# Moving the raw weight loads of a two-level fast matmul from SyncE's DMA queue to ScalarE's

## The chip, the cores and the metric

The kernel runs on one core of one Trainium2 chip. The metric is the device time of one execution in microseconds, as a median over runs. TensorE (PE) multiplies, VectorE (DVE) adds and reads PSUM, ScalarE (ACT) copies out of PSUM and applies relu, GpSimd (POOL) adds in SBUF, SyncE (SP) issues nearly all DMAs. DMAs can also be issued from ACT.

## The reference, cut to what matters

Two residual layers on `x` of shape 2 x 2048 x 512, all in fp32. The first is a mixture: two shared experts and, for each of the two samples, one chosen expert out of five, each 512 to 2048 to 512 with a relu; a softmax gate over three weights, computed from the first token, mixes the three. The second is one chosen 512 x 512 matrix per sample.

```
s0, s1 = relu(x @ swi[0]) @ swo[0], relu(x @ swi[1]) @ swo[1]
h  = relu(einsum('bsd,bdf->bsf', x, wi[type_label]))
eo = einsum('bsf,bfd->bsd', h, wo[type_label])
w  = softmax(relu(concat([eo[:,0], s0[:,0], s1[:,0]]) @ g1) @ g2)
x  = x + eo*w[:,0] + s0*w[:,1] + s1*w[:,2]
x  = x + einsum('bsd,bdh->bsh', x, W[cat_ids]) + b[cat_ids]
```

## The kernel before, in words

**Units.** There are 12 units of work in order: shared expert 0 on four blocks of 1024 tokens, shared expert 1 on the same four blocks, then chosen expert 2 (sample 0) on blocks 0 and 1, and chosen expert 3 (sample 1) on blocks 2 and 3. A unit is an `up` matmul (512 to 2048, line L810) and a `down` matmul (2048 to 512, L945). Both use a seven-product scheme in place of eight, on two levels, so 49 products each. An `up` has 98 slots (seven outer products i, each with seven inner products k in two halves); a `down` has 49. A slot is a few matmuls, the PSUM read that they call for, and whatever background work the slot advances. `clock` counts slots.

**Weight sums.** A product needs sums of weight blocks. For each expert and each of the two matrices (`Prep(e, kind)`, experts 1 to 3, so six of them; expert 0's are made in the first unit) these sums are made once, in four slices. A slice is read as raw weights into the one buffer tagged `raw` (1 MB, eight DMAs of 128 KB, L186); then POOL makes twelve additions (L141) in three lines of four: `o` and `s` read the raw slice, `t` reads `s`. After each addition POOL runs two small memsets (L149). Five slots after a line's fourth addition the line is stored to HBM (`ws_o`, `ws_s`, `ws_t`, L236). The next slice begins when all eight readers of `raw` have been issued and five slots have passed (`free`), and its additions may begin six slots after that (`can`). In an `up` the additions are spread by `RATE_UP` additions a slot, with at most four saved up; in a `down` they go at fixed places (`RUN_DN`), and there POOL first waits for a small DVE memset (`pulse`, L691, and `seen`, L692). `prep_paced` is called once in every slot and counts `clock`.

**Weight tiles.** `fetch_w` loads each product's 256 KB weight tile (`w`) from HBM into twelve rotating buffers. Every load is an SP DMA, issued in program order when a slot has used up a tile: from `ws_t` (L485), `ws_s` (L487), `ws_o` (L489) or the given weights (L494 to L504). The SP queue therefore holds, in one order, the weight tiles, the raw slices, the stores of the sums and the activations' parts.

**Evictions.** A product of the first inner index leaves its PSUM bank by an ACT copy or a DVE addition (`uz`, L825 and L827; `us`, L831 and L833; `h`, L838 to L857), and the next inner product adds to the same bank, so PE has to wait for that read. At places DVE makes wide sums of 128 x 1024 (L787 in `up`, L916 in `down`, L744 to L751 for both).

**Start.** `read_ids` loads the two label vectors by DMA and reads each into an SP register (L91, L93). It stands, in program order, behind the first four transposed pieces of `x` (ACT copies, L286) and the loads of the first weights, and ahead of the first `up`. The whole program is issued in the order it is written; each engine runs its own part in that order.

Of the kernel before, what the change touches and what calls it, by code (L numbers as in the profile page):

```python
# [36 lines left out]
def cond_resid_kernel(  # L37
# [22 lines left out]
    nc = tc.nc  # L60
    B, S, D = x.shape
    E, _, F = wi.shape
    NCAT = W.shape[0]
    NX = g2.shape[1]
    DC = D // P
# [15 lines left out]
    ps = ctx.enter_context(tc.tile_pool(name="ps", bufs=2, space=PSUM))  # L81
    dram = ctx.enter_context(tc.tile_pool(name="dram", bufs=1, space=DRAM))

    label, cat = [], []

    def read_ids():
        ids = const.tile([1, 2, B], type_label.dtype, name="ids")
        nc.sync.dma_start(out=ids[:, 0, :], in_=type_label.rearrange("(o b) -> o b", o=1))
        nc.sync.dma_start(out=ids[:, 1, :], in_=cat_ids.rearrange("(o b) -> o b", o=1))
        for b in range(B):  # L90
            label.append(nc.sync.value_load(ids[0:1, 0, b : b + 1], min_val=0, max_val=E - 1))  # L91
        for b in range(B):
            cat.append(nc.sync.value_load(ids[0:1, 1, b : b + 1], min_val=0, max_val=NCAT - 1))  # L93

# [5 lines left out]
    wi_v = wi.rearrange("e (c p) (r f) -> p (e c) r f", p=P, r=4)  # L100
    swi_v = swi.rearrange("e (c p) (r f) -> p (e c) r f", p=P, r=4)
    wo_v = wo.rearrange("e (r g p) d -> p (e r) g d", p=P, g=NG)
# [28 lines left out]
    def sums_a(eng, pick, put):  # L131


        a11, a12, a21, a22 = pick(0, 0), pick(1, 0), pick(0, 1), pick(1, 1)
        for o, i0, i1, op in (
            (put(5), a21, a22, ADD),
            (put(7), a11, a21, SUB),
            (put(6), put(5), a11, SUB),
            (put(3), a12, put(6), SUB),
        ):  # L140
            eng.tensor_tensor(o, i0, i1, op)  # L141
            yield
# [3 lines left out]
    def rest(count):  # L146

        for _ in range(count):
            nc.gpsimd.memset(idle, 0.0)  # L149

    class Prep:
# [4 lines left out]
        def __init__(self, e, kind):  # L156
# [2 lines left out]
            self.left = {part: NG for part in "ost"}  # L159
            self.p, self.late, self.reading, self.free, self.since = [], [], 0, 0, 0  # L160

        def begin(self):
            if not self.todo:
                return
            g = self.todo.pop(0)
            self.since = clock[0]
            e, kind = self.e, self.kind
            t = bigp.tile([P, 2048], F32, tag="raw", bufs=1, name=f"pr_{e}_{kind}_{g}")

            raw = t.rearrange("p (q b d f) -> p q b d f", q=4, b=2, d=2)  # L170
            cols = slice(g * P, (g + 1) * P)
            for c in range(DC):
                if kind == 0 and e < 2:
                    src = swi_v[:, e * DC + c, :, cols]
                elif kind == 0:
                    src = wi_v[:, bass.ds(label[e - 2] * DC + c, 1), :, cols]
                    src = src.rearrange("p o r f -> p (o r) f")
                elif e < 2:
                    src = swo_v[:, e * 4 + c, g, :].rearrange("p (r f) -> p r f", r=4)
                else:  # L180
                    src = wo_v[:, bass.ds(label[e - 2] * 4 + c, 1), g, :]
                    src = src.rearrange("p o (r f) -> p (o r) f", r=4)
                src = src.rearrange("p (c d) f -> p c d f", c=2)
                a, b = divmod(c, 2)
                for k, q in enumerate((1, 2) if a else (0, 3)):
                    nc.sync.dma_start(out=raw[:, q, b, :, :], in_=src[:, k, :, :])  # L186
            place = lambda n: SLOT_A[n] - 4
            quad = {(0, 0): 0, (1, 0): 1, (1, 1): 2, (0, 1): 3}
            own = {}

            def view(part):
                if part not in own:
                    self.flush(1 << 30, part)
                    own[part] = bigp.tile(
                        [P, 1536 if part == "o" else 2048], F32, tag=part, bufs=1,
                        name=f"p{part}_{e}_{kind}_{g}",
                    )
                form = {
# [3 lines left out]
                }[part]  # L202
                return own[part].rearrange(form, s=4, f=P, **({"b": 2} if part == "s" else {}))

            def line(part, pick, put):
                gen = sums_a(nc.gpsimd, pick, put)

                def op(k):
                    next(gen)
                    rest(2)  # L210
                    if part != "t":
                        self.reading -= 1
                        self.free = clock[0] + 5
                    if k == 3:
                        self.late.append((clock[0] + 5, part, g, own[part]))

                return [lambda k=k: op(k) for k in range(4)]

            self.p += line(
                "o", lambda r, c: raw[:, 0:3, r, c, :], lambda n: view("o")[:, :, place(n), :]  # L220
            )
            self.p += line(
                "s", lambda r, c: raw[:, quad[r, c]], lambda n: view("s")[:, place(n)]
            )
            self.p += line(
                "t", lambda r, c: view("s")[:, :, r, c], lambda n: view("t")[:, :, place(n)]
            )
            self.reading = 8

        def flush(self, now, only="ost"):  # L230
            for job in list(self.late):
# [7 lines left out]
                )  # L239
                self.left[part] -= 1  # L240

        def step(self):

            self.flush(clock[0])
            done = self.can()
            if done:
                self.p.pop(0)()
            self.more()
            return done

        def can(self):
            return bool(self.p) and (len(self.p) != 12 or clock[0] >= self.since + 6)

        def more(self):
            if self.reading == 0 and (not self.p or clock[0] >= self.free):
# [5 lines left out]
        def force(self, part):  # L261
            self.more()
            while self.left[part]:
                if self.p:
                    self.p.pop(0)()
                self.more()
                if not self.p:
                    self.flush(1 << 30)
# [184 lines left out]
    clock = [0]  # L453
# [194 lines left out]
    prep_bg, other_bg = [], []  # L648
# [9 lines left out]
    def prep_step():  # L658
        done = prep_bg[0].step()
        if prep_bg[0].over():  # L660
            prep_bg.pop(0)
        return done
# [3 lines left out]
    def prep_paced(rate):  # L666
        clock[0] += 1
        if prep_bg:
            prep_bg[0].flush(clock[0])
        pace[0] = min(pace[0] + rate, 4.0) if prep_bg else 0.0  # L670
        while prep_bg and pace[0] >= 1 and prep_step():
            pace[0] -= 1
# [81 lines left out]
    def up(n, xg, tops, y):  # L754
# [12 lines left out]
        for j, i in enumerate(I_UP(n)):  # L767
# [32 lines left out]
            for s, (bk, k, d) in enumerate(SEQ_UP):  # L800
# [78 lines left out]
                if s in top_at:  # L879
                    next(tg, None)  # L880
                prep_paced(RATE_UP[n in MAKES][j])
                if n or j or s >= 7:
                    step(other_bg)
# [10 lines left out]
    def down(n, H, tops, y, prepare):  # L894
# [124 lines left out]
        for s, (i, name) in enumerate(SLOTS_DN):  # L1019
            if s in at:  # L1020
                for _ in job:
                    pass
                job = jobs[at[s]]()
                y_sums(0, *sums.get(at[s], ()))
            elif s in second:
                y_sums(1, *sums.get(second[s], ()))
            slot(i, name)
            next(job, None)
            if name == "z2" and i != 1:
                next(job, None)  # L1030
            prepare(s)
            prep_paced(0.0)
            prep_run(RUN_DN[n in MAKES].get((i, name), 0))
            quiet[0] = True
            step(other_bg)
# [220 lines left out]
    def last_layer1(blk, y):  # L1256
# [8 lines left out]


    RATE_UP = [
        [0.36, 0.36, 0.36, 0.36, 0.24, 0.24, 0.36],
        [0.0, 0.24, 0.24, 0.3, 0.3, 0.3, 0.3],
    ]  # L1270
    RUN_DN = [
# [5 lines left out]
    with tc.manual_schedule():  # L1277
# [9 lines left out]
        next(x_rest)  # L1287
        begin = First(y)
        read_ids()
        xg = x_sums(0)  # L1290
        advance(xg)
# [4 lines left out]
        for n, (e, blk) in enumerate(units):  # L1296
# [47 lines left out]
            if e >= 2:  # L1344
                b = e - 2
# [41 lines left out]
```

## Time and profile before

| what | value |
|---|---|
| time, median of 3 runs | 2229.15 us (2228.36 to 2230.01) |
| the profiled execution | 2225.8 us, its span 2224.0 us |
| PE busy / DVE / ACT / POOL | 2184.7 / 1627.8 / 544.3 / 811.9 us |
| moved by DMA | 581.59 MB, 262 GB/s over the span |
| raw slice loads | 192 of 128 KB, all from SP, between 166.0 and 1480 us |
| loads issued from ACT | 25, all of `x` |

Times are microseconds from the span's start. A "waits" row reads: engine and line that waited, what released it, the total, how often, the longest. A timeline row reads: start, duration, engine (SPq and ACTq are the DMA issues of SP and ACT), line, operation, tiles, count, and in brackets the idle time before it with its releaser. A row of the windows reads: stretch, length, busy time and instruction count of PE, weight loads, DVE, ACT and POOL, the granted TensorE clock, the DMA engines' share and GB/s. Unit 0 ends at 212 us, unit 4's `up` begins at 728 us, and the last addition on a weight slice starts in unit 8, at 1548.9 us.

### The profile page before, as it was taken

The numbers are of one execution on the slowest core, as the hardware profiler recorded it, in microseconds if no ns is written. First come the engines' busy times: TensorE is split into PE (matmuls) and PEld (weight loads), VectorE is DVE, ScalarE is ACT, GpSimd is POOL, SyncE is SP. The second block draws the span as 40 slices with busy tenths as digits, with TensorE's granted clock in tenths as the row PEclk, the third lists the DMA queues.
The fourth block names the chain that finished last, engine by engine and source line by source line (L and its number), as shares of the span: only waits on it lengthen the run. The fifth ranks groups of instructions, "written<-read, shape, count | busy, mean of one in ns | idle before, by whom it ended". The sixth has DMA issues, their size and how long they took to land.

```text
span 2224.0 us, 29253 instructions
## 1 busy us (share of the span) xinstructions
PE 2184.7 (98%) x9808; PEld 1851.8 (83%) x9808; DVE 1627.8 (73%) x2047; ACT 544.3 (24%) x937; POOL 811.9 (37%) x1259
## 2 busy tenths in 40 slices
PE   8999999999999999999999999999999999999999
PEld 6787888888888888888888888888877877887785
DVE  7897787687587587588587588588676746867695
ACT  3221231331321321231231141131133133213310
POOL 5887533852840540450450451360033023002400
PEclk9999999999999999999999999999999999999999
DMA  9853997997996996896997997896896697679681
GB/s 341 319 178 98 340 326 218 340 328 233 298 306 211 316 315 200 285 328 185 294 316 223 302 302 236 272 337 205 298 297 192 185 314 237 183 236 318 215 282 52
DMA packets 484256, 581.59 MB, mean 262 GB/s; under 512 B 28552, under 2 KB 316296, under 8 KB 480908
## 3 DMA queue, kind: packets, MB, share of 16 engines
q1 hardware_dynamic: 480380, 572.91, 79.4%
q10 hardware_dynamic: 3728, 6.82, 0.9%
q8 instruction: 80, 1.31, 0.2%
q14 instruction: 68, 0.56, 0.1%
HBM read 421.80 MB, written 157.81 MB: 261 GB/s over the span
## 4 chain that ended last, share of the span: by engine, by line
PE 85%; DVE 7%; DMA 2%; issue 1%; SPq 0%; ACT 0%; DVEq 0%; ACTq 0%
PE dx L945 23%; PE ux L810 23%; PE dy L945 11%; PE uy L810 11%; PE dz L945 6%; PE uz L810 6%; PE po L1159 5%; DVE h L916 1%; DMA w<-ws_t 1%; DVE h L787 1%; DVE t L749 1%; DMA w<-in_L_cond_W_dram 1%; DVE t L747 1%; DVE t L744 1%; DVE t L751 0%
## 5 line engine op out<-in xcount | busy, mean ns | idle before, releaser
L810 PE MATMUL ux<-xs,w 128*128 128x256 f32 x1792 | 426.2, 380 | 10.0 <-DVE uz L827 5.0
L945 PE MATMUL dx<-t,w 128*128 128x256 f32 x1680 | 397.4, 379 | 3.3 <-DVE ds L967 3.1
L810 PEld LDWEIGHTS ux<-xs,w 128*128 128x128 f32 x1792 | 338.9, 190 | 69.8 <-DVE uz L827 8.0
L945 PEld LDWEIGHTS dx<-t,w 128*128 128x128 f32 x1680 | 318.1, 190 | 48.7 <-issue 2.4
L1196 POOL TENSOR_TENSOR mix<-mix 128x512 f32<-128x512 f32 x72 | 110.1, 1531 | 443.0 <-ACT mix L1191 355.3
L833 DVE TENSOR_TENSOR us<-ux,h 128x512 f32<-128x512 f32 x240 | 163.2, 687 | 128.3 <-PE ux L810 128.0
L916 DVE TENSOR_TENSOR h<-h,h 128x1024 f32<-128x1024 f32 x192 | 246.4, 1297 | 0.0
L781 ACT ACTIVATE h<-h 128x1024 f32<-128x1024 f32 x156 | 163.9, 1054 | 235.0 <-DVE h L838 122.4
L810 PE MATMUL uy<-xs,w 128*128 128x256 f32 x896 | 212.5, 380 | 2.1 <-DVE h L857 1.9
L838 DVE TENSOR_TENSOR h<-uy,us 128x512 f32<-128x512 f32 x168 | 116.0, 691 | 119.6 <-ACT us L831 115.5
L692 POOL TENSOR_TENSOR seen<-pulse 1x1 f32<-1x1 f32 x33 | 16.9, 513 | 509.7 <-DVE pulse L691 473.2
L810 PEld LDWEIGHTS uy<-xs,w 128*128 128x128 f32 x896 | 169.7, 190 | 30.0 <-DVE h L857 4.3
L844 ACT ACTIVATE h<-uz 128x512 f32<-128x512 f32 x168 | 99.5, 592 | 351.4 <-PE uz L810 312.2
L945 PE MATMUL dy<-h,w 128*128 128x256 f32 x672 | 159.7, 381 | 4.2 <-DVE y L969 4.1
L810 PE MATMUL ux<-xi,w 128*128 128x256 f32 x640 | 152.2, 380 | 5.1 <-DVE us L833 2.9
L945 PEld LDWEIGHTS dy<-h,w 128*128 128x128 f32 x672 | 127.4, 190 | 22.8 <-issue 5.2
L945 PE MATMUL dx<-h,w 128*128 128x256 f32 x616 | 145.5, 379 | 0.0
L945 PE MATMUL dz<-h,w 128*128 128x256 f32 x616 | 145.5, 379 | 0.0
L857 DVE TENSOR_TENSOR h<-uy,us 128x512 f32<-128x512 f32 x168 | 112.1, 686 | 44.0 <-PE uy L810 42.2
L810 PEld LDWEIGHTS ux<-xi,w 128*128 128x128 f32 x640 | 120.5, 190 | 25.1 <-issue 7.2
L141 POOL TENSOR_TENSOR po<-pr 128x384 f32<-128x384 f32 x48 | 54.5, 1136 | 232.5 <-DMA pr<-in_L_cond_wo_dram 82.4
L787 DVE TENSOR_TENSOR h<-h,h 128x1024 f32<-128x1024 f32 x96 | 135.4, 1410 | 3.2 <-ACT h L844 1.9
(155 smaller groups left out, 3432.9 us busy)
## 6 DMA issues: line engine op xcount, KB each, us to landing
w<-ws_t SPq DMA_DIRECT2D x352, 256.0 KB, 4.2
w<-ws_s SPq DMA_DIRECT2D x270, 256.0 KB, 4.2
w<-ws_o SPq DMA_DIRECT2D x264, 256.0 KB, 4.6
xs<-xs SPq DMA_DIRECT2D x56, 896.0 KB, 7.4
ws_s<-ps SPq DMA_DIRECT2D x24, 1024.0 KB, 8.1
ws_t<-pt SPq DMA_DIRECT2D x24, 1024.0 KB, 9.5
ys<-y SPq DMA_DIRECT2D x11, 2048.0 KB, 7.8
ws_o<-po SPq DMA_DIRECT2D x24, 768.0 KB, 6.6
```

Source lines behind the costliest of these rows:

```text
L141: eng.tensor_tensor(o, i0, i1, op)
L781: nc.scalar.activation(v, v, AF.Relu)
L787: nc.vector.tensor_tensor(o, blk_of(O[22], cc), blk_of(O[21], cc), ADD)
L810: nc.tensor.matmul(p[:, g, :], lhsT=wt[:, 2 * d + g, :], rhs=x_ops[n, i, k], start=first and g == 0, stop=True, skip_group_check=True,)
L833: nc.vector.tensor_tensor(t, p, half(src, 12 if k == 6 else 22, d), ADD)
L838: nc.vector.tensor_tensor(half(dst, 22, d), bank["y", d], t, ADD)
L844: nc.scalar.activation(half(dst, 11, d), p, AF.Relu if i in final else AF.Copy)
L857: nc.vector.tensor_tensor(half(dst, 12, d), p, sn["b", d], ADD)
L916: nc.vector.tensor_tensor(bl(o), bl(i0), bl(i1), SUB)
L945: nc.tensor.matmul(p, lhsT=wt[:, g, :], rhs=op[g], start=first and g == 0, stop=True, skip_group_check=True,)
L1159: nc.tensor.matmul(po[t], lhsT=mixed[c], rhs=l1[blk][0][:, c, :], start=(c == 0), stop=(c == DC - 1),)
L1196: nc.gpsimd.tensor_tensor(m[:, 3, :, :], m[:, 3, :, :], m[:, j, :, :], ADD)
```

## The change

The eight loads of every slice are no longer issued when the slice begins. They are put on a list, and `prep_paced` issues one of them in each slot, from ACT's DMA queue. This goes for the slices of shared expert 1 as for those of the chosen experts. Because the addresses depend on the labels, ACT reads the type labels into registers of its own at the start. A slice's additions may begin once the list is empty and four slots have passed since its last load. `RATE_UP` rises by 0.02 from unit 4 on (its first row; units 1 to 3 use the second, which stays).

```diff
     def read_ids():
...
         for b in range(B):
-            label.append(nc.sync.value_load(ids[0:1, 0, b : b + 1], min_val=0, max_val=E - 1))
+            of = ids[0:1, 0, b : b + 1]
+            label.append(nc.sync.value_load(of, min_val=0, max_val=E - 1))
+            label_act.append(nc.scalar.value_load(of, min_val=0, max_val=E - 1))
...
         def begin(self):
...
-                    src = wi_v[:, bass.ds(label[e - 2] * DC + c, 1), :, cols]
+                    src = wi_v[:, bass.ds(label_act[e - 2] * DC + c, 1), :, cols]
...
-                    src = wo_v[:, bass.ds(label[e - 2] * 4 + c, 1), g, :]
+                    src = wo_v[:, bass.ds(label_act[e - 2] * 4 + c, 1), g, :]
...
                 for k, q in enumerate((1, 2) if a else (0, 3)):
-                    nc.sync.dma_start(out=raw[:, q, b, :, :], in_=src[:, k, :, :])
+                    self.loads.append((raw[:, q, b, :, :], src[:, k, :, :]))
...
+        def load(self):
+            if self.loads:
+                o, v = self.loads.pop(0)
+                nc.scalar.dma_start(out=o, in_=v)
+                self.since = clock[0]
...
         def can(self):
-            return bool(self.p) and (len(self.p) != 12 or clock[0] >= self.since + 6)
+            if len(self.p) == 12:
+                return not self.loads and clock[0] >= self.since + 4
+            return bool(self.p)
...
         def force(self, part):
             self.more()
             while self.left[part]:
+                while self.loads:
+                    self.load()
...
     def prep_paced(rate):
         clock[0] += 1
         if prep_bg:
             prep_bg[0].flush(clock[0])
+            prep_bg[0].load()
...
     RATE_UP = [
-        [0.36, 0.36, 0.36, 0.36, 0.24, 0.24, 0.36],
+        [0.38, 0.38, 0.38, 0.38, 0.26, 0.26, 0.38],
         [0.0, 0.24, 0.24, 0.3, 0.3, 0.3, 0.3],
     ]
```

More of the change, by code (lines that the diff above doesn't have):

```diff
@@ L82, in cond_resid_kernel @@
     dram = ctx.enter_context(tc.tile_pool(name="dram", bufs=1, space=DRAM))
-    label, cat = [], []
+    label, label_act, cat = [], [], []
     def read_ids():
@@ L160, in __init__ @@
             self.p, self.late, self.reading, self.free, self.since = [], [], 0, 0, 0
+            self.loads = []
         def begin(self):
```

## The prediction

> **What bounds the kernel now.** I began with the page's busy shares and the chain that ended last, from which these lines are taken.
>
> ```profile
> PE 2184.7 (98%) x9808; PEld 1851.8 (83%) x9808; DVE 1627.8 (73%) x2047; ACT 544.3 (24%) x937; POOL 811.9 (37%) x1259
> ...
> PE 85%; DVE 7%; DMA 2%; issue 1%; SPq 0%; ACT 0%; DVEq 0%; ACTq 0%
> ```
>
> PE is the bound: no change of loads can bring more than PE's idle time, 2224.0 - 2184.7 = 39.3 us, and only the part near the moved loads. So I cut the span at the borders of the stages (columns as in the table's notes).
>
> ```profile
> 0.00:212.00 212.00, 191.44 (x852) 160.10 (x853) 182.08 (x183) 54.87 (x103) 154.39 (x141) 0.98 0.68 240
> 212.00:728.00 516.00, 515.53 (x2418) 452.67 (x2417) 376.65 (x484) 128.70 (x230) 251.30 (x476) 1.00 0.87 284
> 728.00:1510.00 782.00, 771.82 (x3558) 673.85 (x3557) 577.46 (x721) 188.91 (x309) 292.07 (x565) 1.00 0.88 281
> ```
>
> PE is idle 20.6 us in unit 0, 0.5 us in units 1 to 3 (9 of the 24 slices are loaded up to there, at no cost) and 10.2 us from 728 us to 1510 us, where the other loads lie. PE's waits in that last stretch:
>
> ```profile
> PE ux L810 <- DVE uz L827: 3.5, 5, 1.1
> PE ux L810 <- DMA w<-ws_t: 2.3, 2, 1.9
> PE ux L810 <- DMA w<-in_L_cond_swi_dram: 2.2, 1, 2.2
> PE uy L810 <- DVE h L857: 1.9, 2, 1.1
> ```
>
> 4.5 us are late weight tiles, 5.4 us are late DVE evictions. One of the late tiles, first on SP's queue, then on PE:
>
> ```profile
> 938.94 0.52 SPq L236 DMA_DIRECT2D ws_s<-ps  x1
> 939.67 10.10 SPq L186 DMA_DIRECT2D pr<-in_L_cond_wo_dram  x8
> 949.87 0.38 SPq L485 DMA_DIRECT2D w<-ws_t  x1
> ```
>
> ```profile
> 953.63 0.67 PE L810 MATMUL ux<-xs,w 128*128 128x256 f32 x2 [1.92 <-DMA w<-ws_t]
> ```
>
> The tile is issued only when the eight raw loads have left SP, and PE waits for it. The bursts before the other two late tiles (0.4 us at 783.3, 2.2 us at 1135.1) also held SP about 10 us: from 769.5 to 779.6 and from 1115.9 to 1125.6.
>
> **What leaves SP.** A burst that nothing obstructs takes SP 4.15 us (1475.89, eight issues with a median of 0.33 us and what lies between). In a 10 us burst the other 6 us are its first issue (6.29 us at 939.67), and that wait belongs to the 1 MB store ahead of it: where a tile stands behind such a store it has it too (w<-ws_o, 6.50 us at 953.80, behind ws_t<-pt). So this part stays on SP and goes to the next tile; about 4.1 us a burst leave. The three tiles were late by 0.4, 1.9 and 2.2 us, less than 4.1 each. Gain 4.5 us, between 0 (the bytes, not the issue, are late) and 4.5.
>
> The Trainium skill speaks against the change here: "DMA: Bandwidth & Descriptors", under "Issuing engines are not separate DMA queues", says that DMAs from any engine share the same 16 DMA engines and that a second issuer saves only the issuing time. The DMA share of 0.88 beside the 10 us burst agrees that the engines are nearly full; by the strictest reading of the rule the tiles land as late as before and this term would be 0, by the issue rows it is 4.5.
>
> **What ACT gets.** 192 loads and some register instructions. The nearest row is ACT's own loads of `x`: 24 issues, 0.334 to 0.444 us, median 0.335, so 192 x 0.335 = 64 us on an engine that is busy 24%. They need not wait for SP's blocked queue:
>
> ```profile
> 318.72 4.02 SPq L487 DMA_DIRECT2D w<-ws_s  x1
> ...
> 322.46 0.33 ACTq L300 DMA_DIRECT2D xn<-in_x_dram  x1
> ```
>
> A load stands behind its slot's eviction and runs while that is computed; what is queued behind it is the next slot's eviction, and PE waits for that. 16 of the 24 `x` issues lie in the stretch in which PE lost 0.5 us in all, so at most 0.03 us each, 192 x 0.03 = 5.6 us; below nothing is excluded, since an issue frees no eviction. I take 0, as those issues cost nothing by themselves.
>
> The first load of a slice also waits on ACT until POOL has read the old slice, and the evictions would wait behind it. SP's stores of the sums wait for POOL in the same way: 28.1 us in 26 times, the longest 5.2 us. A slice begins five slots after the last reader is issued and its first load goes one slot later. An `up` slot is 0.865 us (the chain has eight matmuls, two slots, in 1.73 us), six are 5.2 us: as long as the longest wait. So 0; without that cover 28.1 us at most.
>
> **Additions.** The eight loads now leave over eight slots, 6.9 us, and the additions begin four slots later, twelve slots behind the slice's begin instead of six. The row's 0.02 more an `up` slot makes up for it: counting slots by the code, the last store falls in the same slot of unit 8. What moves is where POOL's run of additions lies. It matters to DVE: the wide sum L787 takes 1.22 us alone and up to 2.26 us beside POOL, and this is where the 5.4 us of DVE waits come from (mostly in the outer products i = 7 and i = 4 of units 4 to 8). After the change the runs lie some ten slots earlier in units 4 to 6 and later in unit 8. I see no reason for fewer or for more: 0, between -5.4 (no meeting) and +5.4 (twice as many).
>
> **The start.** The labels reach SP late, and ACT will now wait for the same DMA. In order: SP's label reads, ACT, PE, and PE's clock (before the last column but one).
>
> ```profile
> L91 SPq TENSOR_LOAD <-ids x2: 281/376/471, 18.8 to 19.6; - x2
> ```
>
> ```profile
> 9.93 0.66 ACT L286 ACTIVATE x<-pt 128x256 f32<-128x256 f32 x2 [0.20 <-PE pt L337]
> 11.14 0.58 ACT L825 ACTIVATE uz<-ux 128x512 f32<-128x512 f32 x1 [0.56 <-PE ux L810]
> ```
>
> ```profile
> 13.53 1.89 PE L810 MATMUL ux<-xi,w 128*128 128x256 f32 x8
> ...
> 28.32 1.22 PE L810 MATMUL uy<-x,w 128*128 128x256 f32 x2 [5.96 <-DVE h L838]
> ```
>
> ```profile
> 24.12:27.54 3.42, 0.00 (x0) 0.00 (x0) 3.42 (x3) 0.00 (x0) 3.42 (x5) 1.00 1.02 407
> 27.54:30.95 3.41, 2.63 (x6) 2.18 (x7) 3.04 (x6) 1.45 (x2) 3.33 (x5) 0.50 1.01 407
> ```
>
> The reads stand on ACT behind the copy at 9.93 and ahead of the eviction at 11.14. The labels are there at 18.8 and two reads end at 20.2, so `uz` ends at about 20.8 and PE's matmul of 13.53, which adds to that bank, starts at 20.9: 7.4 us late. But PE later waits 6.0 us until 28.32 for DVE, whose work up to there (sums of the first weights) needs nothing of ACT. PE's work from 13.53 to 22.35 takes 8.8 us and would end at 29.7 instead of 28.32: +1.4. The clock is halved from 27.54 to 34.36 after the idle stretch (the stretch from 30.95 has 0.50 too), which costs (34.36 - 28.32)/2 = 3.0 us; with the idle time earlier that half clock comes earlier and costs 1.6 us (until 24.12) to 3.3 us (until 27.54). Sum 1.4 - 3.0 + 1.6 to 3.3 = 0.0 to +1.7; I take +1.0. Bounds: -1.6 with no half clock at all, and +10.4 (7.4 and another 3.0) if nothing is absorbed.
>
> "TensorE: Matmul & The Clock Gate", Part 1, gives free-running windows of 3413 ns and full clock after one busy window. The rows' stretch of 3.41 us agrees; yet the half clock here lasted two such stretches, though PE was busy 2.63 of 3.41 us in the first. By the page's rule the start would cost 0.0, by two stretches +1.7.
>
> **Sum.** -4.5 + 0 + 0 + 0 + 1.0 = -3.5 us: the profiled execution's 2225.8 us become 2222.3. The median of the runs stands 3.35 us above that execution, so 2225.7 us for the median. The measurement tells about 0.2%, 4.5 us, from no change, so this forecast counts as the same.
>
> **Rivals.**
>
> - Faster: the shifted additions also miss DVE's wide sums, and all 9.9 us of waits from 728 to 1510 us go. 2229.15 - 9.9 + 1.0 = 2220.3. For it: the runs of units 4 and 5 leave i = 4. Against: they lie over i = 5 and i = 7 instead, where unit 7's run (1281 to 1301 us) cost PE a wait, too.
> - Slower: ACT's wait for the labels at the start is not absorbed. -4.5 + 10.4 = +5.9, 2235.1 us. For it: DVE is busy 182 of 212 us in unit 0, and POOL's `x` sums, which need ACT, move 7 us into DVE's later work. Against: the 6.0 us wait just behind. It decides once the start costs over 9.0 us (4.5 + 4.5).
> - No gain, the change does not do what it says: SP's 6 us wait behind the stores and the full DMA engines keep the tiles late. +1.0, 2230.2 us. For it: the tile issued at 1127.12 took 7.9 us to land. Against: the burst ahead of it is what filled that queue.
>
> **How the numbers follow.** Forecast 0.52, faster rival 0.16, slower rival 0.20, no gain 0.12. The forecast's own range is 2221 to 2231 (its DVE and start terms), 0.20 of it below 2224.7 and 0.32 above. Faster: 0.20 + 0.16 = 0.36. Same: 0.32 + 0.12 = 0.44. Slower: 0.20. The range takes in both outer rivals' centres, 2219.5 to 2235.5; beyond lie the tails of these two and the 28.1 us of ACT behind POOL.
>
> **What would show it.** Right: PE's waits on `w` from 728 to 1510 us gone; raw loads as ACTq rows of about 0.35 us; ACT's first `uz` near 20 us, with PE idle from 13.5 to 20.9 and not before 28; unit 1 starting within 2 us of 212.1. Wrong: ACTq rows of microseconds or waits of ACTq on POOL with PE waiting for ACT; unit 1 starting over 4 us late; DVE waits above 10 us.

## The result and the profile after

The changed kernel takes 2265.94 us, the median of five runs (2259.98 to 2270.66), against 2229.15 us for the kernel before: a ratio of 1.0166, 95% interval 1.0151 to 1.0182. The forecast was 2225.7 us, the range 2219.5 to 2235.5. The change is slower by 37 us and lies 30 us above the range. The profiled execution took 2270.66 us, its span 2268.9 us, 44.9 us longer than the span before. That is the slowest of the five runs, while the profiled execution before was 3.35 us below its median: the differences of the profiles below add up to 8 us more than those of the medians.

Cut at the borders of the stages, as in the prediction (columns: stretch, length, busy time with instruction count of PE, weight loads, DVE, ACT and POOL, granted clock, DMA share, GB/s):

```profile
0.00:214.10 214.10, 191.34 (x853) 160.27 (x854) 178.69 (x183) 54.86 (x103) 154.35 (x140) 0.98 0.66 233
214.10:747.80 533.70, 521.92 (x2418) 455.01 (x2417) 378.34 (x483) 128.76 (x230) 249.09 (x473) 0.99 0.86 276
747.80:1631.60 883.80, 862.61 (x3921) 748.47 (x3920) 634.81 (x793) 197.01 (x330) 304.75 (x574) 0.99 0.84 267
```

Unit 0 is 2.1 us longer than before, units 1 to 3 are 17.7 us longer (516.00 before), units 4 to 8 are 23.1 us longer (860.7 before, from 728.0 to 1588.7 us), the rest is 2.0 us longer. PE is busy for 6.4 us more in the second stretch and 12.1 us more in the third with practically the same instructions, and idle for 11.3 and 11.0 us more. The busy part is the clock: apart from the span's last few us, PE ran at half clock for 10.2 us before (from 27.5 and 157.2 us) and for 41.0 us after, in pieces of 3.41 or 6.83 us. The added pieces begin at 469.2, 639.9, 793.5, 971.0, 1148.4 and 1510.3 us, all but the last at a stall of PE of 2.7 to 4.8 us. Half of 41.0 - 10.2 is 15.4 us lost to the clock.

PE's waits in units 4 to 8 (the same part of the program as in the prediction's list), and then in units 1 to 3:

```profile
PE ux L826 <- ACT us L847: 12.3, 9, 3.6
PE ux L826 <- DVE uz L843: 5.0, 10, 1.1
...
PE ux L826 <- ACT uz L841: 1.7, 1, 1.7
```

```profile
PE uy L826 <- POOL xi L399: 4.8, 1, 4.8
PE uy L826 <- POOL idle L152: 2.9, 1, 2.9
PE dx L961 <- ACT ds L981: 1.7, 2, 1.5
```

(L826, L841, L843, L847, L873 and L399 are L810, L825, L827, L831, L857 and L384 of before; POOL's additions are L144, its small memsets L152.) The late weight tiles are gone, as forecast: no row on `w` is left. In their place PE waits 14.0 us for ACT, which did not appear in this list before, and in units 1 to 3 for POOL's sums of `x` and, 3.0 us in all, for ACT.

One of the waits for ACT, on SP's queue, on ACT and on PE:

```profile
1141.69 0.42 SPq L363 DMA_DIRECT2D xs<-xs  x1
```

```profile
1144.87 3.80 ACTq L250 DMA_DIRECT2D pr<-in_L_cond_wi_dram  x2
1148.72 0.60 ACT L847 ACTIVATE us<-ux 128x512 f32<-128x512 f32 x1 [5.95 <-DMA pr<-in_L_cond_wi_dram]
```

```profile
1149.37 2.93 PE L826 MATMUL ux<-xs,w 128*128 128x256 f32 x6 [3.55 <-ACT us L847]
```

Two loads take 3.80 us of ACT's queue, although one issue takes 0.38 us. In the trace each DMA names the semaphore that it raises when it lands. SP's and ACT's DMAs have eight of them, in turn and in program order over both queues, and a DMA is not issued before the earlier one with its semaphore has landed. The second load here shares its semaphore with SP's load `xs` of 1141.69, which lands at 1148.28; the load is issued at 1148.30, the eviction behind it runs at 1148.72 and PE goes on at 1149.37. I paired every DMA with its predecessor in this way and counted it as held where it stood over 0.15 us and left within 0.25 us of that landing. 47 of the 192 loads were held, 67.9 us in all and 4.6 us at most: over a third of it by ACT's own earlier loads, the rest by SP's DMAs. SP's queue goes by the same rule: its weight tiles were held for 49.9 us before (71 of 1091) and for 145.7 us after (100), 51.8 us of it by the loads on ACT.

Not every wait for ACT is of this kind. Of the 14.0 us, 11.5 come after held loads. The other 2.5 us, five waits between 1108.6 and 1292.4 us, come after loads of which none was held. There the issue just ahead of the eviction took 1.09 to 1.42 us, and the eviction starts 0.05 us after its end. 37 of the 192 issues took over 0.5 us; why, no run shows. One of these waits, on ACT and on PE:

```profile
1106.51 1.42 ACTq L250 DMA_DIRECT2D pr<-in_L_cond_wo_dram  x1
1107.98 0.60 ACT L847 ACTIVATE us<-ux 128x512 f32<-128x512 f32 x1 [1.05 <-PE uz L826]
```

```profile
1108.63 1.13 PE L826 MATMUL ux<-xs,w 128*128 128x256 f32 x4 [0.33 <-ACT us L847]
```

POOL around 464 us, and PE behind it:

```profile
463.84 1.01 POOL L144 TENSOR_TENSOR po<-pr 128x384 f32<-128x384 f32 x1 [18.62 <-DMA w<-ws_o]
...
469.54 0.72 POOL L399 TENSOR_TENSOR xi<-x 128x256 f32<-128x256 f32 x1
```

```profile
470.32 3.78 PE L826 MATMUL uy<-xi,w 128*128 128x256 f32 x8 [4.83 <-POOL xi L399]
```

The slice's eight loads left ACT from 445.9 to 458.2 us. POOL stands at its first addition until 463.84 (the row names the landing that came last by the profile, a tile's; in e3 below the same place names the raw loads), makes four additions, and only then the sum `xi` that PE needs; eight matmuls, 1.89 us otherwise, take 3.78 us at half clock behind it.

### The profile page after: what moved, and what is told of

It is laid out like the page before. It is cut to its first block, busy times and chain, and to the rows that moved or that the text cites. A ratio compares the mean times of both kernels' runs of the same rounds, so it can differ in the third digit from the quotient of the medians.

```text
span 2268.9 us, 29294 instructions
## 1 busy us (share of the span) xinstructions
PE 2203.5 (97%) x9808; PEld 1859.6 (82%) x9808; DVE 1626.1 (72%) x2046; ACT 545.1 (24%) x937; POOL 817.1 (36%) x1258
## 4 chain that ended last, share of the span: by engine, by line
PE 76%; DVE 8%; DMA 5%; POOL 3%; issue 1%; ACTq 1%; ACT 0%; SPq 0%; POOLq 0%; DVEq 0%
PE dx L961 22%; PE ux L826 19%; PE dy L961 11%; PE uy L826 8%; PE dz L961 5%; PE uz L826 5%; PE po L1175 5%; DVE h L803 2%; DMA pr<-in_L_cond_wi_dram 1%; DVE h L932 1%; DVE t L765 1%; DMA w<-in_L_cond_W_dram 1%; DMA w<-ws_t 1%; DVE t L763 1%; DVE h L873 1%
## 5 line engine op out<-in xcount | busy, mean ns | idle before, releaser
L826 PE MATMUL ux<-xs,w 128*128 128x256 f32 x1792 | 435.4, 385 | 21.4 <-ACT us L847 12.7
L826 PEld LDWEIGHTS ux<-xs,w 128*128 128x128 f32 x1792 | 342.9, 193 | 87.1 <-ACT us L847 19.5
L1212 POOL TENSOR_TENSOR mix<-mix 128x512 f32<-128x512 f32 x72 | 108.9, 1514 | 445.9 <-ACT mix L1207 278.1
L826 PE MATMUL uy<-xs,w 128*128 128x256 f32 x896 | 212.9, 380 | 2.1 <-DVE h L873 1.9
L826 PEld LDWEIGHTS uy<-xs,w 128*128 128x128 f32 x896 | 169.4, 190 | 30.9 <-DVE h L873 5.2
L826 PE MATMUL ux<-xi,w 128*128 128x256 f32 x640 | 156.1, 387 | 14.2 <-POOL idle L152 9.0
L826 PEld LDWEIGHTS ux<-xi,w 128*128 128x128 f32 x640 | 123.0, 194 | 35.8 <-POOL idle L152 10.8
L144 POOL TENSOR_TENSOR po<-pr 128x384 f32<-128x384 f32 x48 | 57.1, 1189 | 263.6 <-DMA pr<-in_L_cond_wo_dram 55.7
L873 DVE TENSOR_TENSOR h<-uy,us 128x512 f32<-128x512 f32 x168 | 112.0, 686 | 45.7 <-PE uy L826 43.9
```

The source lines that it names most:

```text
L826: nc.tensor.matmul(p[:, g, :], lhsT=wt[:, 2 * d + g, :], rhs=x_ops[n, i, k], start=first and g == 0, stop=True, skip_group_check=True,)
L873: nc.vector.tensor_tensor(half(dst, 12, d), p, sn["b", d], ADD)
L1212: nc.gpsimd.tensor_tensor(m[:, 3, :, :], m[:, 3, :, :], m[:, j, :, :], ADD)
```

## Experiments

The columns of units are differences of the profiled execution to that of before, in us; the median is over the timed runs, and the ratio is to the kernel before on the same chip, whose medians there were 2225.4 to 2229.2 us. The profiled execution can lie some us from the median (for e11 and e12 it was the fastest of the runs, 4 and 8 us below).

| kernel | loads from, how | median us | ratio (95%) | unit 0 | 1 to 3 | 4 to 8 | 9 to 11 |
|---|---|---|---|---|---|---|---|
| changed | ACT, one a slot | 2265.94 | 1.0166 (1.0151 to 1.0182) | 2.2 | 17.7 | 23.2 | 2.0 |
| e1 | SP, one a slot | 2263.24 | 1.0164 (1.0144 to 1.0184) | 1.4 | 17.9 | 17.4 | -0.4 |
| e2 | before + label reads | 2231.91 | 1.0027 (1.0016 to 1.0037) | 0.9 | 2.0 | -0.9 | 1.2 |
| e4 | before + tiny DMAs | 2253.57 | 1.0108 (1.0082 to 1.0134) | 0.5 | 10.3 | 17.2 | 0.9 |
| e8 | ACT, burst | 2306.96 | 1.0353 (1.0334 to 1.0371) | 3.1 | 34.0 | 47.6 | 0.1 |
| e3 | POOL, one a slot | 2245.26 | 1.0082 (1.0066 to 1.0099) | 7.8 | 13.2 | -2.0 | 0.6 |
| e7 | SP, burst; late additions | 2229.67 | 1.0007 (0.9995 to 1.0020) | -1.1 | 3.3 | 2.9 | 0.9 |
| e5 | ACT; additions 12 slots behind | 2277.33 | 1.0222 (1.0205 to 1.0239) | 3.4 | 5.1 | 13.4 | 30.3 |
| e12 | ACT; 12 slots in units 0 to 3 | 2262.38 | 1.0159 (1.0143 to 1.0174) | 2.2 | 4.4 | 15.8 | 6.0 |
| e14 | ACT for chosen experts only | 2242.43 | 1.0078 (1.0063 to 1.0094) | 2.2 | 1.7 | 12.6 | 0.6 |
| e11 | POOL, one a slot; 12 slots | 2242.00 | 1.0069 (1.0055 to 1.0084) | -1.4 | 14.7 | -6.7 | 6.0 |
| e10 | POOL, burst | 2230.72 | 1.0019 (1.0009 to 1.0029) | -0.9 | 9.8 | -4.5 | 0.9 |
| e13 | POOL burst, chosen experts only | 2221.85 | 0.9985 (0.9976 to 0.9994) | -1.0 | 1.3 | -5.7 | 0.3 |

**e1: the changed kernel with the queue put back** (and without ACT's label reads).

```diff
-                nc.scalar.dma_start(out=o, in_=v)
+                nc.sync.dma_start(out=o, in_=v)
```

> The kernel after, with its raw loads issued from SP, still one a slot, and without the label reads on ACT. If ACT's queue is the cause (its evictions stand behind loads that wait), PE's 14.0 us of waits on ACT go and the start's 2 us with them: 2228 to 2240 us, the upper part if the units with x sums on POOL keep their loss. If the spreading and the later additions are the cause, whichever queue is used: 2260 us or more.

ACT as the issuer is not the whole cause: PE's waits for ACT go and the time stays. PE waits 9.9 us for `xi` in units 1 to 3 instead, and for late weight tiles, which now stand on SP behind loads that are held there: 24 of the 192 loads, 16.3 us (before, 4 and 5.5 us). The time is the one expected if the spread of the loads were the cause; e3 below speaks against that in units 4 to 8.

**e2: the kernel before with ACT's label reads alone.**

```diff
+            label_act.append(nc.scalar.value_load(of, min_val=0, max_val=E - 1))
```

> The kernel before, with ACT's two label reads at the start alone, which nothing uses. By the start of the kernel after (unit 1 began 2.0 us later than before): 2231 us, with ACT's first eviction at about 20 us. If the wait is not absorbed: 2236 us or more.

The label reads cost 5.2 us by the medians (3.6 to 8.2 by the interval) and 3.0 us by the profiles, of the change's 37.

**e4: the kernel before with eight DMAs of eight bytes a slice from ACT, one a slot,** and nothing else changed.

```diff
+        def load(self):
+            if self.loads:
+                k = self.loads.pop(0)
+                nc.scalar.dma_start(out=tiny[:, k, :], in_=g1[k : k + 1, 0:2])
...
     def prep_paced(rate):
...
+            prep_bg[0].load()
```

> The kernel before, its raw loads on SP as they were, and beside them eight DMAs of 8 bytes per slice from ACT, one a slot, whose data nothing uses. They move nothing and depend on no reader of the raw slice; what they share with the loads of the kernel after is only that every DMA waits for the DMA eight places ahead of it in program order, whose completion semaphore it takes over. If that wait on ACT is the cause: PE waits on ACT's evictions for 8 us or more from unit 4 on, 2237 to 2260 us. If the cause is the bytes, the readers of the raw slice or the issue time: 2229 to 2232 us.

No bytes to speak of, no raw load moved, no addition moved, and still 27 us. ACT is held at 49 of these 192 DMAs, 54.0 us in all, the longest 4.8 us, and SP's tiles are held for 96.0 us (49.9 before). Each of PE's six waits for ACT in units 1 to 8, 10.2 us, comes behind a tiny DMA that was held; what the free issues (0.23 us in the median) cost beside that is not separated. Each further DMA also brings a predecessor eight places back closer in time. PE's waits for ACT's evictions and for late tiles show both sides:

```profile
PE dx L954 <- ACT ds L974: 4.3, 3, 2.7
...
PE ux L819 <- DMA w<-ws_s: 3.9, 4, 2.2
```

**e8: the kernel before with only the queue changed,** bursts of eight from ACT, with the label reads there.

```diff
-                    nc.sync.dma_start(out=raw[:, q, b, :, :], in_=src[:, k, :, :])
+                    nc.scalar.dma_start(out=raw[:, q, b, :, :], in_=src[:, k, :, :])
```

> The kernel before with only the queue changed: the eight loads of a slice leave in one burst from ScalarE (with the label reads on ScalarE), additions six slots behind the begin and rates as before. Theory A (each load waits for the DMA eight places before it, and evictions stand behind it on ScalarE): a burst of 4 to 10 us stands ahead of the next evictions in each of 24 slices, PE can cover about one slot of 0.87 us in the two banks, so 24 x 3 to 9 us and half clock on top: over 2290 us. Theory B (the queue costs little and the spread costs): 2229 to 2240 us.

The worst of all, with fewer held loads than in the changed kernel (40, 46.2 us): a burst is one long block in front of the next eviction, held or not. ACT and PE at one of them:

```profile
771.68 5.96 ACTq L191 DMA_DIRECT2D pr<-in_L_cond_wi_dram  x8
777.68 1.08 ACT L847 ACTIVATE us<-ux 128x512 f32<-128x512 f32 x2 [5.86 <-DMA pr<-in_L_cond_wi_dram]
```

```profile
778.33 3.78 PE L826 MATMUL ux<-xs,w 128*128 128x256 f32 x8 [4.61 <-ACT us L847]
```

None of these eight loads waited for its predecessor, which had landed: the block is their own issues, 0.38 us each but two of 1.16 and 1.17 us, and 0.2 us between them. So plain issue time has a price too where eight issues stand together ahead of an eviction, and the sum of the held time is not the whole price.

**e3: the changed kernel with loads and label reads on POOL's queue.** In this program those DMAs use semaphores of their own and wait for no other queue's DMA.

```diff
-                nc.scalar.dma_start(out=o, in_=v)
+                nc.gpsimd.dma_start(out=o, in_=v)
```

> The changed kernel with the 192 loads (and the label reads) issued from GpSimd's queue in place of ScalarE's; slots, additions and rates as in the changed kernel. In the program these loads then wait for no completion semaphore of the other queues' DMAs. Theory A (a load holds its queue until the DMA eight places before it in the program has landed, and evictions or tiles stand behind it): units 4 to 8, which lost 23.6 us, lose under 6 us, PE's waits for ACT's us fall from 13.3 us to under 2 us; units 1 to 3 keep most of their 17.7 us, since POOL's additions stand where they stood: about 2248 us, between 2240 and 2256. Theory B (the spread of the loads over eight slots and the later additions cost by themselves, whatever the queue): units 4 to 8 lose over 15 us as they did from ScalarE's and SyncE's queues: 2260 us or more. If an issue on POOL takes about a microsecond, POOL gets 192 us more and its x sums come late: then DVE's and PE's waits for POOL rise, over 2270 us.

Same slots, same additions, and units 4 to 8 lose nothing (-2.0 us against +23.2): the spread of the loads costs nothing there by itself. (The 7.8 us in unit 0 go in e11, where POOL reads the labels later.) PE's waits from 744 to 1540 us, where ACT and the tiles no longer appear:

```profile
PE ux L826 <- DVE uz L843: 4.9, 7, 1.2
PE uy L826 <- DVE h L873: 3.1, 4, 1.0
```

Units 1 to 3 still lose 13.2 us, and here the releaser of POOL's addition is named plainly:

```profile
467.34 1.00 POOL L144 TENSOR_TENSOR po<-pr 128x384 f32<-128x384 f32 x1 [6.13 <-DMA pr<-in_L_cond_swo_dram]
```

The 13.2 us need not be that wait alone: in e10 POOL's own issues cost these units 9.8 us with the additions where they were before.

**e7: the additions where the change has them, the loads as before.**

```diff
-            return bool(self.p) and (len(self.p) != 12 or clock[0] >= self.since + 6)
+            return bool(self.p) and (len(self.p) != 12 or clock[0] >= self.since + 12)
```

(and the change's `RATE_UP`).

> The kernel before with its bursts of eight loads from SyncE, but with the additions where the change puts them: twelve slots behind the slice's begin in place of six, and the change's rates for up rows (0.38 and 0.26). Theory A (units 1 to 3 lose 17.7 us because POOL stands at an addition whose loads have not landed, with the x sums behind it): in a burst all eight loads leave by the second slot, the additions come ten slots later and find the data there, so no unit loses over 3 us: 2226 to 2234 us. Theory B (the place of the additions among POOL's x sums and DVE's wide sums is what costs): units 2 and 3 lose 4 to 9 us each as in the changed kernel, 2240 to 2255 us.

No measurable difference by the medians. The prediction's zero for the place of the additions holds as long as their loads have landed.

**e5 and e12: later additions.** In e5 every slice's additions begin twelve slots behind its last load, in e12 those of shared expert 1 alone (loaded in units 0 to 3):

```diff
-                return not self.loads and clock[0] >= self.since + 4
+                return not self.loads and clock[0] >= self.since + (12 if self.e == 1 else 4)
```

> The kernel after, with a slice's additions twelve slots behind its last load instead of four. If POOL, standing at an addition whose raw data has not landed with the x sums behind it, is the cause in units 1 to 3: their PE waits on POOL (4.8 and 2.9 us) go with the half clock behind them, 2250 to 2260 us; the waits on ACT in units 4 to 8 stay. If not: 2262 to 2270 us.

> The changed kernel (loads one a slot from ScalarE, labels read there at the start) with one edit: for the slices of units 0 to 3 the additions begin twelve slots behind the last load in place of four; the others keep four. Theory A (POOL stood at additions whose loads had not landed): units 2 and 3 give back 8 to 12 us with the half clock behind their waits, units 4 to 8 keep their 23.6 us: 2253 to 2259 us. Theory B (units 1 to 3 lose by ScalarE's waits as the others do): under 4 us come back, 2262 us or more.

Units 1 to 3 give back 12.6 and 13.3 of their 17.7 us, so most of that loss was POOL's standing: in the changed kernel PE's 7.7 us of waits for POOL and the half clock there (5.1 us) make 12.8. In e5, PE's matmul that stood at 470.32 runs at 467.02 without a wait. The totals do not follow. e5 is slower than the changed kernel, 2277.33 us against the 2250 to 2260 expected: the last sums are not ready at the end of unit 8, and PE waits once for 26.9 us at the start of unit 9, with 27.3 us of half clock behind it. In e12 the median gains only 3.6 us, which by itself is what theory B expected; the profiled execution, with a span 16.8 us shorter than the changed kernel's, was the fastest of its runs and shows the gain of theory A in units 1 to 3, as e5's does. In it the shift has moved all later loads against the tiles, and unit 6's `down` to unit 9's `up` lose 26.9 us in place of units 4 to 6. That also shows when a held load is free: of the eight loads below the sixth was held for 3.0 us. In unit 4 of e12, ACT and PE:

```profile
756.88 7.23 ACTq L250 DMA_DIRECT2D pr<-in_L_cond_wi_dram  x8
```

```profile
758.53 1.89 PE L826 MATMUL ux<-xs,w 128*128 128x256 f32 x8
760.25 1.89 PE L826 MATMUL uy<-xs,w 128*128 128x256 f32 x8
```

ACT does nothing but issue for 7.2 us and PE loses nothing: no eviction of ACT's is due in these slots. In the `up` parts of units 4 to 6 the loads are held on ACT for about as long in both kernels (between 25 and 30 us), yet the changed kernel loses 17.1 us there and e12 gains 4.7.

**e14: the changed kernel with the chosen experts' loads alone on ACT;** shared expert 1's stay in bursts on SP with additions six slots behind.

```diff
-                    self.loads.append((raw[:, q, b, :, :], src[:, k, :, :]))
+                    if e >= 2:
+                        self.loads.append((raw[:, q, b, :, :], src[:, k, :, :]))
+                    else:
+                        nc.sync.dma_start(out=raw[:, q, b, :, :], in_=src[:, k, :, :])
```

> The changed kernel with the loads one a slot from ScalarE for the routed experts' slices alone; the slices before them leave in bursts from SyncE with additions six slots behind, as in the kernel before (rates and the label reads at the start as in the changed kernel). Theory A (two separate losses, one in units 1 to 3 by POOL's additions and one later by ScalarE's waits): units 1 to 3 lose under 3 us, the start 1 to 2 us, the later units lose 17 to 28 us between them, though perhaps in other units than in the changed kernel, since the slots of the loads against the tiles shift: 2246 to 2258 us. Theory B (the losses of the later units follow from what units 1 to 3 leave late): under 2238 us.

The two losses are separate: units 1 to 3 are as before within 1.7 us and the later ones still lose 12.6 us. That is less than the 17 to 28 us expected, and the median lies below the 2246 us that the range began with. Here only 6.8 us of half clock fall in units 4 to 8, against 20.5 us in the changed kernel, which makes 6.8 us of the difference; the rest may be the place of the held loads, as in e12, but no run separates it.

**e11, e10 and e13: POOL's queue put to use.** Each label is read on POOL ahead of the first load that needs it. e11 is e3 with that and with e12's twelve slots; e10 is the kernel before with the bursts on POOL; e13 moves the bursts of the chosen experts only:

```diff
+            if e >= 2 and e - 2 not in label_pool:
+                label_pool[e - 2] = nc.gpsimd.value_load(label_at[e - 2], min_val=0, max_val=E - 1)
...
-                    nc.sync.dma_start(out=raw[:, q, b, :, :], in_=src[:, k, :, :])
+                    (nc.gpsimd if e >= 2 else nc.sync).dma_start(out=raw[:, q, b, :, :], in_=src[:, k, :, :])
```

> The changed kernel with the loads one a slot on GpSimd's queue, the labels read there only when first needed, and for the slices of units 0 to 3 the additions twelve slots behind the last load in place of four. If the three causes (labels read at the start, loads waiting on shared completion semaphores, POOL standing at additions whose slice has not landed) are all, it gives back 7 us in unit 0 and over 8 of the 13.2 us that units 1 to 3 lose from GpSimd's queue at four slots: 2225 to 2232 us. If the spread of the loads has a price of its own, it stays over 2238 us.

> The kernel before with only the queue of the raw loads changed: a burst of eight from GpSimd's queue at the slice's begin, additions six slots behind and rates as before; each label is read on GpSimd just ahead of the first load that needs it, not at the start. Theory A: no load holds SyncE's or ScalarE's queue and none waits on a shared completion semaphore; POOL issues eight loads in about 4.3 us (0.54 us each), which it has time for. The late tiles (4.5 us) go, the rest stays: 2219 to 2228 us. Theory B (the DMA engines' bytes set when the tiles land, not the issue): 2226 to 2232 us, with the waits for tiles as before. Theory C (POOL's x sums behind the bursts come late in units 1 to 3): units 1 to 3 lose over 3 us, 2232 us or more.

> The kernel before with the queue changed for the routed experts' slices alone (15 of the 24 are loaded in units 4 to 8): bursts of eight from GpSimd's queue, each label read there when first needed; the other slices stay in bursts on SyncE; additions and rates as before. Theory A (GpSimd's queue costs only where POOL has x sums to make, units 1 to 3, and spares units 4 to 8 the late tiles): units 4 to 8 run 3 to 5 us shorter, the others as before: 2221 to 2226 us, faster than both kernels. Theory B (the tiles land no earlier on the whole; the 4.6 us seen there are scatter): 2226 to 2231 us.

e11 misses its number: units 4 to 8 gain 6.7 us, but unit 3's `down` loses 8.0 us behind one DVE wait of 5.8 us, and unit 9 loses 5.9 us. I did not settle why; the later additions may crowd into unit 3's `down`, as they do into unit 9 in e5. Its rival, a price of the spread itself in units 1 to 3, is not excluded by it. e10 falls between its theories: units 4 to 8 gain 4.5 us, units 1 to 3 lose 9.8 us, where POOL's eight issues of a slice stand ahead of the `x` sums; PE waits 3.6 us for `xi`, the rest of the 9.8 I did not trace. e13 keeps the gain without that loss and is faster than both kernels, 3.3 us by the ratio, with an interval of 1.3 to 5.3 us. PE's waits in the stretch of the prediction's list, 728 to 1510 us:

```profile
PE ux L828 <- DVE uz L845: 3.3, 6, 0.8
PE uy L828 <- DVE h L875: 1.8, 3, 1.0
```

## Why the prediction was wrong

**What leaves SP: right.** The three late tiles, 4.5 us, are gone in the changed kernel and in e13, whose interval of 1.3 to 5.3 us holds 4.5. (The DMA share of 0.88 given beside the 10 us burst is the mean of the whole stage; from 940 to 955 us it was 0.99.) The step by which the burst's 4.1 us, and not the bytes, made the tiles late holds. The Trainium skill ("DMA: Bandwidth & Descriptors", under "Issuing engines are not separate DMA queues"), by which another issuer saves the issuing time alone, fits e13's small gain; the strict reading, a term of 0, does not.

**What ACT gets: wrong, the main failure.** The prediction wrote of the loads that "They need not wait for SP's blocked queue", and took 0 because "16 of the 24 `x` issues lie in the stretch in which PE lost 0.5 us in all". The median issue was near right, 0.34 to 0.46 us by kind of load; the sum was not, 97.8 us in place of 64, of which the 37 long issues are 39.8. Above all the loads do wait for SP's DMAs, through the shared completion semaphores. The row quoted for it (an ACT issue of 0.33 us beside a blocked SP) was one case in which the predecessor had landed; the `x` loads were 24 and only 3 of them were held, 2.1 us in all. From 25 DMAs a price for 192 was read, while SP's own tiles, held for 49.9 us at 71 issues, were the row that carried it. A held load then stands in front of an eviction, and the term had 5.6 us at most for all of it. Units 4 to 8 lose 23.2 us instead, of which half clock is 10.2 us (20.5 us at half speed).

**The wait on POOL: sized too simply.** Loads that stood for something else than a predecessor on their semaphore, POOL's reads of the old slice mostly, did so for some 11 us in all, the longest 5.4 us, against the 28.1 us named as the bound. What PE lost by these alone was not separated; behind the two longest, at 625.9 and 1308.2 us, PE shows no wait for ACT.

**Additions: wrong for a reason that the step did not look at.** It weighed POOL against DVE's wide sums and found 0 within 5.4 us; e7 confirms that. The loss is on POOL itself, which works in order: the twelve slots were counted in program order, but held loads left later than their slots (445.9 to 458.2 us for eight slots of 0.87 us) and took 4.9 us to land in the median, 3.1 before. Four slots, 3.5 us, do not cover that, and in units 1 to 3 the `x` sums stand behind. 17.7 us, of which e12 gives back 13.3.

**The start: the way right, the size too small.** `uz` was to end at 20.8 us and PE to go on at 20.9:

```profile
20.18 1.07 ACT L841 ACTIVATE uz<-ux 128x512 f32<-128x512 f32 x2 [9.77 <-issue]
```

```profile
20.86 3.75 PE L826 MATMUL ux<-xi,w 128*128 128x256 f32 x8 [6.59 <-POOL idle L152]
```

Later PE does not wait for DVE's `h` any more (6.0 us before). But unit 1 starts 2.0 us late, where 0.0 to 1.7 and +1.0 were forecast, and e2, which has this term alone, is 5.2 us slower by the medians. Where the part beyond unit 0 arises was not traced. The half clock lasted two stretches again, from 18.6 to 25.4 us.

**The rivals.** The slower one put its price at the start, which cost 2.0 us in the profile. None was a DMA issue on ACT that waits for something else than its data. The sign named for being wrong, ACTq rows of microseconds with PE waiting for ACT, is the one that came. And no term gave a stall the half clock behind it, which was priced for the start only: 15.4 of the 44.9 us.

## What to carry to other kernels

Before a DMA is moved to the queue of an engine that computes, look at which semaphore it raises and what used that one before: here a DMA on SP's or ACT's queue was issued only when that earlier DMA had landed, on whichever of the two, and everything behind it on the engine waited too. Price it by the held issues of the busiest queue, not by the median of a few free ones, count the issues that stand together, and ask which of the engine's outputs is due next. An addition placed a fixed number of slots behind a load needs the load's landing time in those slots, or it holds all else on its engine.

## What the runs showed of the hardware that was not expected

Eight-byte DMAs, one a slot from ACT, cost 27 us without moving data (e4). Loads from POOL's queue took POOL 0.54 to 0.72 us each in the median by kind and cost units 4 to 8 nothing (-2.0 us in e3).

A stall of about 3 us costs more than itself. Around the one at 793 us, by windows of 3.41 us (the granted clock is the last column but two):

```profile
790.10:793.51 3.41, 1.29 (x5) 0.68 (x4) 0.15 (x1) 0.26 (x1) 0.00 (x0) 0.99 1.06 355
793.51:796.92 3.41, 2.69 (x6) 2.19 (x7) 0.61 (x1) 2.15 (x4) 0.00 (x0) 0.50 0.83 265
796.92:800.34 3.42, 3.42 (x10) 2.70 (x9) 2.00 (x3) 1.42 (x3) 0.00 (x0) 0.51 1.10 312
800.34:803.75 3.41, 3.41 (x17) 3.02 (x16) 1.92 (x2) 0.62 (x2) 1.84 (x4) 1.00 0.99 334
```

PE stood for 2.1 us of the first window; the next two ran at half clock, though PE was busy throughout the second of them. The 2.7 us wait thus cost another 3.4 us. "TensorE: Matmul & The Clock Gate", Part 1, of the Trainium skill gives full clock after one busy window; that agrees if the window from 793.51 us, idle for 0.7 us of it, doesn't count as busy.
